# Two convolution layers by involution: which tiles of a column are multiplied 64 channels at a time, and which queue issues the window copies

## The chip, the core and the metric

The kernel runs on one core of a Trainium2 chip. A core has five engines with a queue each: TensorE (PE, matrix products; its weight loads are shown apart as PEld), VectorE (DVE), ScalarE (ACT), GpSimd (POOL) and SyncE (SP, which here only issues DMA transfers). Each engine works through its instructions in program order and waits on semaphores for the others. Products are written to PSUM, which is used here as four pairs of banks of 512 float32 per partition. The metric is the device time of one execution in microseconds; less is better.

## The reference

The input is 4 images of 256 channels and 56 x 56 points. Four residual layers follow, each on a group-normalised input. The change touches the code of layers 0 and 2, which are involutions: every point has its own 7 x 7 kernel, shared by the 16 channels of a group, which is itself computed from the input.

```python
def _L0_conv_ref(x, reduce_w, reduce_b, span_w, span_b):
    patches = jax.lax.conv_general_dilated_patches(x, (K, K), (S, S), [(P, P), (P, P)])
    patches = patches.reshape(b, G, c // G, K * K, Ho, Wo)
    ...
    h = jnp.einsum('bchw,oc->bohw', xk, reduce_w) + reduce_b[None, :, None, None]
    kern = jnp.einsum('bchw,oc->bohw', h, span_w) + span_b[None, :, None, None]
    kern = kern.reshape(b, G, 1, K * K, Ho, Wo)
    out = (kern * patches).sum(axis=3)
    return out.reshape(b, c, Ho, Wo)
...
x = x + _L0_conv_ref(_gn(x), ...)
x = x + _L1_conv_ref(_gn(x), ...)
x = x + _L2_conv_ref(_gn(x), ...)
x = x + _L3_conv_ref(_gn(x), ...)
```

Layer 2 computes the same with a batch norm and a ReLU after the reduction and after the sum. Layer 1 is two 3 x 3 convolutions, layer 3 a gate by channel and by position.

## The kernel before

The three stages of the time are the first involution (to about 508 us of the span), the convolutions (to about 1250 us), and the second involution with the gates of layer 3 worked in between (to the end). The function `involution_layer` is run twice, with `layer` 0 and 2.

**Units and columns.** An involution goes through 8 units: 4 images by 2 blocks of 128 channels (the partitions). A unit first makes its tap matrices (`tap_matrices`, 32 groups of products at line 596, evicted to `kt` by DVE at line 615 and, each third, by ACT at line 608), and then goes through 7 columns, each 8 points wide and 56 high.

**Tiles.** A column is cut into 19 tiles of 3 x 8 = 24 points (the last has rows below the image). The input window of a tile is 9 x 14 = 126 points. With the window's points on the partitions, the involution of a tile is a product of `xw` (126 window points by channels) with `kt` (126 window points by 24 outputs, for each of 8 groups of 16 channels). As the groups have different taps, a product of 64 channels with the taps of 4 groups computes 4 x 24 values for each channel, of which only the 24 of its own group are wanted; one of 32 channels with 2 groups computes 2 x 24. A tile needs two products of 64 channels and 96 free elements, or four of 32 channels and 48 free elements. The wanted values are picked in the eviction, by as many passes as a product has groups: the first by ACT with a per-partition factor that is 1 or 0 (times the batch norm's scale in layer 2), the others by DVE, which add into the same tile `un` (line 657).

**`apply` (lines 625 to 664)** does a column by the table `O_PARTS`, two pairs of banks. The first pair has 5 tiles in each bank by products of 64 channels (30 rows of the image): 20 products, one ACT pass of 240 elements (line 650 in layer 0, 652 in layer 2), three DVE passes of 240. The second pair uses one bank, 9 tiles by products of 32 channels (26 rows): 36 products, one ACT and one DVE pass of 208. After each pair the result is added to the image: by POOL in layer 0 (line 662), by DVE with the ReLU in layer 2 (line 664).

**The windows.** For a column, a strip of the normalised image is written to `strip_sb` (POOL in layer 0, line 390; ACT in layer 2, line 388), PE transposes it in 7 pieces (line 405), ACT copies these to `xw` (line 417), and four DMA transfers copy `xw` to itself, shifted by 3 and by 6 rows, so that all 19 windows stand there (lines 423 and 425). SP issues all four in layer 2; in layer 0, POOL issues the second of the shift by 6 rows. `xw` has three buffers.

**The order** of each engine's instructions is the order of the program (`in_order`). In a unit's column loop it is: the column's products and evictions (`apply`), the transposes, copy and DMA transfers of a later column's windows (`next_windows`), the strip after that (`next_strip`), the statistics of the column before (line 1115), and pieces of other work placed by column: statistics of the next image (line 358) and the bottleneck products of the next image (line 468) in layer 0, and in layer 2 loads and POOL work of the gates. SP also issues the loads of the next images.

Of the kernel before, what the change touches and what calls it, by code (L numbers as in the profile page):

```python
# [10 lines left out]
F32 = mybir.dt.float32  # L11
AF = mybir.ActivationFunctionType
ALU = mybir.AluOpType
# [3 lines left out]
P = 128  # L17
B, C, H, W = 4, 256, 56, 56
# [5 lines left out]
G, GC = 16, 16  # L24
# [9 lines left out]
TY, TX = 3, 8  # L34
QY, QX = TY + KK - 1, TX + KK - 1
Q = QY * QX
NTY, NTX = -(-H // TY), W // TX
NT = NTY * NTX
TP = TY * TX
# [7 lines left out]

O_PARTS = ((4, (0, 5), 5, 30), (2, (10,), 9, 26))  # L50
NXW = 3


# [18 lines left out]
def net_kernel(  # L72
# [19 lines left out]
    nc = tc.nc  # L92
# [64 lines left out]
    bn = {}  # L157
# [141 lines left out]
    def involution_layer(layer, xin, xout, red, span, sb, xs_of, ahead=None, pending=None):  # L299

        with ExitStack() as es:
            wpool = es.enter_context(tc.tile_pool(name="iw", bufs=1))
            big = es.enter_context(tc.tile_pool(name="ibig", bufs=1))
            work = es.enter_context(tc.tile_pool(name="iwork", bufs=2))
            banks = es.enter_context(tc.tile_pool(name="banks", bufs=4, space=PSUM))

            def two_banks():

                return banks.tile([P, 2, 512], F32, name="ps")
# [82 lines left out]
            def window(ty):  # L392

                k, j = divmod(ty, TY)
                return (0, NSB, 2 * NSB - 1)[j] + k
# [3 lines left out]
            def begin_windows():  # L399

                flat = strips[len(xws)].rearrange("p h w -> p (h w)")
                ps = two_banks().rearrange("p i n -> p (i n)")
                begun_windows.append(ps)
                for k in range(NSB):
                    nc.tensor.transpose(ps[:Q, k * P : (k + 1) * P], flat[:, k * Q : (k + 1) * Q], ident_sb)  # L405

            def next_windows():

                if len(xws) == len(columns):
                    return  # L410
                if not begun_windows:
                    begin_windows()
                ps = begun_windows.pop()
                xw = work.tile([Q, NTY, P], F32, name="xw", bufs=NXW)
                xws.append(xw)

                nc.scalar.copy(xw[:, :NSB, :], ps[:Q, : NSB * P].rearrange("q (n c) -> q n c", n=NSB))  # L417

                n = NSB - 1
                for j in range(1, TY):  # L420
                    cut = TY * QX * j
                    at = window(j)
                    nc.sync.dma_start(xw[: Q - cut, at : at + n, :], xw[cut:Q, 0:n, :])
                    eng = nc.sync if layer == 2 or j == 1 else nc.gpsimd
                    eng.dma_start(xw[Q - cut : Q, at : at + n, :], xw[:cut, 1 : 1 + n, :])


            h_of = {}
# [196 lines left out]
            def apply(b, cb, kt, tx, xw):  # L625

                img = xs_of[b, cb].rearrange("p (h w) -> p h w", w=W)
                y0 = 0
                for ng, tys, nty, rows in O_PARTS:
                    pair = two_banks()  # L630
                    nb, m = len(tys), ng * GC
                    v = pair[:, :nb, : ng * nty * TP].rearrange("p i (e n) -> p i e n", e=ng)
                    for i in range(nb):
                        for k in range(nty):
                            ty = tys[i] + k
                            for j in range(P // m):
                                nc.tensor.matmul(  # L637
                                    v[m * j : m * j + m, i, :, k * TP : (k + 1) * TP],
                                    xw[:, window(ty), m * j : m * j + m],
                                    kt[:, ng * j : ng * j + ng, :, ty * NTX + tx, :],  # L640
                                    start=True,
                                    stop=True,
                                )
                    n = rows // nb * TX
                    o = [v[:, :, e, :n] for e in range(ng)]
                    un = work.tile([P, 2, O_PARTS[0][3] // 2 * TX], F32, name="un")
                    un = un.rearrange("p i n -> p (i n)")[:, : rows * TX]
                    part = un.rearrange("p (i n) -> p i n", i=nb)
                    if layer == 0:
                        nc.scalar.mul(part, o[0], bn["par"][ng][:, 0:1])  # L650
                    else:
                        nc.scalar.activation(  # L652
                            part, o[0], AF.Identity, bias=bn["t4"][:, cb : cb + 1], scale=bn["s4"][ng][:, 0, cb : cb + 1]
                        )
                    for e in range(1, ng):
                        s = bn["par"][ng][:, e : e + 1] if layer == 0 else bn["s4"][ng][:, e, cb : cb + 1]
                        nc.vector.scalar_tensor_tensor(part, o[e], s, part, ALU.mult, ALU.add)  # L657
                    dst = img[:, y0 : y0 + rows, tx * TX : (tx + 1) * TX]
                    y0 += rows
                    u = un.rearrange("p (r x) -> p r x", x=TX)  # L660
                    if layer == 0:
                        nc.gpsimd.tensor_tensor(dst, u, dst, ALU.add)  # L662
                    else:
                        nc.vector.scalar_tensor_tensor(dst, u, 0.0, dst, ALU.max, ALU.add)
# [304 lines left out]
            if layer == 0:  # L969
                place(hooks0, begin(), (1, 2, 4, 6, 7))  # L970
            else:
                since = mark()
                load_taps(0)
                nc.sync.dma_start(zb_sb, zb2_dram)
                next_strip()
                run(bottleneck(0))
                hooks0[3] = list(pending[0])
                for _ in range(NXW - 1):
                    next_windows()
                    next_strip()  # L980
                hooks0[7] = [next_windows, next_strip]
            if layer == 0:
                next_strip()
                for i in range(NXW):
                    hooks0.setdefault(2 + 5 * i, []).extend((next_windows, next_strip))
# [40 lines left out]
            for u, (b, cb) in enumerate(units):  # L1026
# [24 lines left out]
                if b + 1 < B:  # L1051
                    n = 16 if layer == 0 else (26, 21)[cb]
# [64 lines left out]
                for tx in range(NTX):  # L1117
                    if layer == 2 and u == len(units) - 1 and tx == NTX - 1:
                        column_sums(tx - 1)
                    for f in early[tx]:  # L1120
                        f()
                    apply(b, cb, kt, tx, xws[u * NTX + tx])
                    next_windows()
                    next_strip()
                    if tx > 0 and not (layer == 2 and u == len(units) - 1 and tx == NTX - 1):
                        column_sums(tx - 1)
                    for f in late[tx]:
                        f()
# [3 lines left out]
            b, cb, st, last_sums = prev  # L1132
# [636 lines left out]
```

## Time and profile before

| | |
|---|---|
| median of 3 runs | 1797.18 us (1792.46 to 1799.98) |
| the profiled execution, device time | 1791.96 us |
| its span, first to last instruction | 1790.2 us |
| mean granted TensorE clock | 0.983 |
| products of `apply` (L637) | 12,544 records, 340.4 us busy |
| eviction passes of DVE (L657) | 448, 102.5 us (layer 2) and 98.2 us (layer 0) |
| eviction passes of ACT (L652, L650) | 224, 59.6 us (layer 2) and 50.0 us (layer 0) |
| the copies `xw<-xw` | 392 issued by SP, 56 by POOL |

The profile is one execution, and the device time is 1.8 us more than its span. Times are in us, means of one instruction in ns. A float32 product is shown as two records of PE, and each has a weight load under PEld. In a row of the groups stand line, engine, operation, tile written and tiles read, their shapes, the number, the busy time, the mean of one, and behind the bar the engine's idle time before them and who ended it; "issue" is idle time for which the profile shows no wait. Matmuls are pipelined, so that the duration of one (about 0.2 us) is far above the step from one to the next.

### The profile page before, as it was taken

The numbers are of one execution on the slowest core, as the hardware profiler recorded it, in microseconds if no ns is written. First come the engines' busy times: TensorE is split into PE (matmuls) and PEld (weight loads), VectorE is DVE, ScalarE is ACT, GpSimd is POOL, SyncE is SP. The second block draws the span as 40 slices with busy tenths as digits, with TensorE's granted clock in tenths as the row PEclk, the third lists the DMA queues.
The fourth block names the chain that finished last, engine by engine and source line by source line (L and its number), as shares of the span: only waits on it lengthen the run. The fifth ranks groups of instructions, "written<-read, shape, count | busy, mean of one in ns | idle before, by whom it ended". The sixth has DMA issues, their size and how long they took to land.

```text
span 1790.2 us, 55795 instructions
## 1 busy us (share of the span) xinstructions
PE 1682.8 (94%) x24040; PEld 1469.8 (82%) x24040; DVE 1387.3 (77%) x2745; ACT 822.8 (46%) x1882; POOL 406.8 (23%) x627
## 2 busy tenths in 40 slices
PE   6999999999989999999999999999999899799887
PEld 4887888878878988898889888986887787688775
DVE  2777787776779988998899888985777687677675
ACT  2655556555642313231323122113768577577564
POOL 2224432344310000000000000001000464563572
PEclk9999999999989999999999999999999999999997
DMA  2445444644752112120112011122446667766753
GB/s 86 128 158 172 148 145 134 188 121 130 222 158 91 55 52 64 64 68 29 64 64 70 26 64 37 44 111 74 153 147 186 186 219 210 215 213 178 203 145 119
DMA packets 69043, 221.04 MB, mean 123 GB/s; under 512 B 13461, under 2 KB 23198, under 8 KB 65086
## 3 DMA queue, kind: packets, MB, share of 16 engines
q1 hardware_dynamic: 52302, 150.65, 27.1%
q0 software_dynamic: 14656, 64.77, 11.4%
q8 instruction: 190, 3.11, 0.7%
q10 hardware_dynamic: 1840, 2.05, 0.4%
q14 instruction: 55, 0.45, 0.1%
HBM read 80.91 MB, written 49.81 MB: 73 GB/s over the span
## 4 chain that ended last, share of the span: by engine, by line
PE 64%; DVE 20%; ACT 5%; issue 4%; DMA 4%; POOL 2%; SPq 1%; POOLq 0%; ACTq 0%; DVEq 0%
PE mm L1533 18%; PE ps L596 15%; PE ps L637 9%; PE mm L1451 9%; DVE kt L615 5%; PE mm L1422 5%; DVE un L657 4%; DMA xw<-xw 3%; PE ps L405 2%; PE ps L468 1%; ACT kt L608 1%; DVE st L1115 1%; DVE res L1526 1%; POOL strip_sb L390 1%; DVE xs L1385 1%
## 5 line engine op out<-in xcount | busy, mean ns | idle before, releaser
L596 PE MATMUL ps<-hp,z_sb 64*126 64x133 f32 x6144 | 387.6, 280 | 8.4 <-DVE kt L615 4.2
L637 PE MATMUL ps<-kt,xw 126*32 126x48 f32 (+1 forms) x12544 | 340.4, 223 | 53.3 <-issue 37.5
L596 PEld LDWEIGHTS ps<-hp,z_sb 64*126 64x126 f32 x6144 | 364.7, 186 | 27.7 <-DVE kt L615 6.2
L1533 PE MATMUL mm<-v,u_sb 128*128 128x280 f32 (+1 forms) x1728 | 383.5, 383 | 1.9 <-DVE u_sb L1264 1.5
L637 PEld LDWEIGHTS ps<-kt,xw 126*32 126x32 f32 (+1 forms) x12544 | 302.7, 118 | 99.4 <-issue 71.2
L615 DVE TENSOR_TENSOR kt<-ps,zb_sb 126x798 f32<-126x798 f32 x352 | 332.8, 980 | 63.8 <-PE ps L596 63.2
L1533 PEld LDWEIGHTS mm<-v,u_sb 128*128 128x128 f32 x1728 | 326.1, 189 | 56.3 <-DVE u_sb L1264 1.9
L608 ACT ACTIVATE kt<-ps,zb_sb 126x133 f32<-126x133 f32 x960 | 290.1, 492 | 101.0 <-PE ps L596 101.0
L1451 PE MATMUL mm<-v,u_sb 128*128 128x252 f32 (+1 forms) x936 | 209.7, 384 | 0.0
L1451 PEld LDWEIGHTS mm<-v,u_sb 128*128 128x128 f32 x936 | 176.5, 190 | 30.6 <-issue 0.8
L657 DVE SCALAR_TENSOR_TENSOR un<-ps,s,un 128x240 f32<-128x240 f32 x224 | 102.5, 458 | 90.6 <-ACT un L652 86.2
L1570 POOL DMA_DIRECT2D x<-xs x24 | 13.2, 549 | 680.1 <-DVE xs L1569 426.5
L657 DVE SCALAR_TENSOR_TENSOR un<-ps,par_sb,un 128x240 f32<-128x240 f32 x224 | 98.2, 456 | 77.7 <-ACT un L650 73.4
L1518 ACT ACTIVATE res<-xs,shift,norm_sb 128x1120 f32<-128x1120 f32 (+1 forms) x24 | 30.2, 1258 | 238.5 <-DVE xs L1569 107.3
L405 PE MATMUL ps<-ident_sb,strip_sb 128*126 128x128 f32 x784 | 113.2, 286 | 16.4 <-POOL strip_sb L390 10.5
L417 ACT COPY xw<-ps 126x896 f32<-126x896 f32 x112 | 101.4, 907 | 51.8 <-PE ps L405 43.3
L662 POOL TENSOR_TENSOR xs<-un,xs 128x240 f32<-128x240 f32 x112 | 72.3, 665 | 180.7 <-DVE un L657 180.5
L405 PEld LDWEIGHTS ps<-ident_sb,strip_sb 128*126 128x126 f32 x784 | 86.0, 143 | 28.0 <-POOL strip_sb L390 17.9
L652 ACT ACTIVATE un<-ps,bn_t,s 128x240 f32<-128x240 f32 x112 | 59.6, 538 | 101.4 <-PE ps L637 97.3
L1422 PE MATMUL mm<-xs,u_sb 128*128 128x126 f32 (+1 forms) x792 | 98.7, 277 | 2.1 <-DVE xs L1385 1.0
L650 ACT ACTIVATE un<-ps,par_sb 128x240 f32<-128x240 f32 x112 | 50.0, 448 | 104.0 <-PE ps L637 92.1
L1422 PEld LDWEIGHTS mm<-xs,u_sb 128*128 128x128 f32 x792 | 94.4, 191 | 3.5 <-DVE xs L1438 1.6
(256 smaller groups left out, 1905.8 us busy)
## 6 DMA issues: line engine op xcount, KB each, us to landing
xw<-xw SPq DMA_DIRECT2D x168, 252.0 KB
xw<-xw SPq DMA_DIRECT2D x224, 126.0 KB
xw<-xw POOLq DMA_DIRECT2D x56, 252.0 KB, 4.6
xs<-x SPq DMA_DIRECT2D x24, 560.0 KB
x<-xs POOLq DMA_DIRECT2D x8, 1568.0 KB
xs<-x SPq DMA_DIRECT2D x8, 1568.0 KB
xs<-in_x_dram SPq DMA_DIRECT2D x6, 1568.0 KB
x<-xs SPq DMA_DIRECT2D x6, 1568.0 KB
```

The lines of the kernel that those rows point to most:

```text
L405: nc.tensor.transpose(ps[:Q, k * P : (k + 1) * P], flat[:, k * Q : (k + 1) * Q], ident_sb)
L417: nc.scalar.copy(xw[:, :NSB, :], ps[:Q, : NSB * P].rearrange("q (n c) -> q n c", n=NSB))
L596: nc.tensor.matmul(ps[:Q, i, k * NT : (k + 1) * NT], z_sb[i * R : (i + 1) * R, cb * GB + g if layer == 0 else g, z0 : z0 + Q], hp[i * R : ...
L608: nc.scalar.activation(kt[:, g, pb, :, p], ps[:Q, i, k * NT : (k + 1) * NT], AF.Identity, bias=zb[:, p : p + 1],)
L615: nc.vector.tensor_tensor(kt[:, g, pb].rearrange("q t (i k) -> q t i k", i=2), ps[:Q, :, : PR * NT].rearrange("q i (k t) -> q t i k", k=PR ...
L637: nc.tensor.matmul(v[m * j : m * j + m, i, :, k * TP : (k + 1) * TP], xw[:, window(ty), m * j : m * j + m], kt[:, ng * j : ng * j + ng, :, ...
L652: nc.scalar.activation(part, o[0], AF.Identity, bias=bn["t4"][:, cb : cb + 1], scale=bn["s4"][ng][:, 0, cb : cb + 1])
L657: nc.vector.scalar_tensor_tensor(part, o[e], s, part, ALU.mult, ALU.add)
L662: nc.gpsimd.tensor_tensor(dst, u, dst, ALU.add)
L1422: nc.tensor.matmul(ps[:, co * m : (co + 1) * m], u[ci][:, co * P : (co + 1) * P], v2[:, e, : n // 2, ci * WT : (ci + 1) * WT], start=(ci = ...
L1451: nc.tensor.matmul(ps, u1_sb[:, ci, dy, k, co * P : (co + 1) * P], v[:, k, dy * NB + ci : (dy + n - 1) * NB + ci + 1 : NB, :], start=(j == 0),
L1533: nc.tensor.matmul(ps, u2_sb[:, ci, dy, k, co * P : (co + 1) * P], v[:, k, dy * NB + ci : (dy + n - 1) * NB + ci + 1 : NB, :], start=(j == 0),
```

## The change

`O_PARTS` now gives each bank of each pair as (groups of a product, first tile, tiles). The first pair is as before. The second pair has four tiles by products of 64 channels in its first bank and five by products of 32 in the second. A column has 28 products of 64 channels and 20 of 32, where it had 20 and 36. Where the two banks of a pair are alike they are evicted together; the second pair's are evicted one after the other, ACT once and DVE three times on 96 elements, then ACT and DVE once each on 120. The addition to the image remains one for each pair. In layer 0 the copy that POOL issued is issued by SP.

```diff
-O_PARTS = ((4, (0, 5), 5, 30), (2, (10,), 9, 26))
+O_PARTS = (((4, 0, 5), (4, 5, 5)), ((4, 10, 4), (2, 14, 5)))
...
-                    eng = nc.sync if layer == 2 or j == 1 else nc.gpsimd
-                    eng.dma_start(xw[Q - cut : Q, at : at + n, :], xw[:cut, 1 : 1 + n, :])
+                    nc.sync.dma_start(xw[Q - cut : Q, at : at + n, :], xw[:cut, 1 : 1 + n, :])
...
-                y0 = 0
-                for ng, tys, nty, rows in O_PARTS:
+                for banks_of in O_PARTS:
                     pair = two_banks()
-                    nb, m = len(tys), ng * GC
-                    v = pair[:, :nb, : ng * nty * TP].rearrange("p i (e n) -> p i e n", e=ng)
-                    for i in range(nb):
+                    for i, (ng, ty0, nty) in enumerate(banks_of):
+                        m = ng * GC
+                        v = pair[:, i, : ng * nty * TP].rearrange("p (e n) -> p e n", e=ng)
                         for k in range(nty):
-                            ty = tys[i] + k
+                            ty = ty0 + k
                             for j in range(P // m):
                                 nc.tensor.matmul(
-                                    v[m * j : m * j + m, i, :, k * TP : (k + 1) * TP],
+                                    v[m * j : m * j + m, :, k * TP : (k + 1) * TP],
                                     xw[:, window(ty), m * j : m * j + m],
                                     kt[:, ng * j : ng * j + ng, :, ty * NTX + tx, :],
...
-                    n = rows // nb * TX
-                    o = [v[:, :, e, :n] for e in range(ng)]
-                    un = work.tile([P, 2, O_PARTS[0][3] // 2 * TX], F32, name="un")
+                    tiles = sum(nty for _, _, nty in banks_of)
+                    rows = min(tiles * TY, H - y0)
+                    un = work.tile([P, 10 * TP], F32, name="un")
+                    same = banks_of[0][::2] == banks_of[1][::2]
+                    at = 0
+                    for i, (ng, _, nty) in enumerate(banks_of[:1] if same else banks_of):
+                        nb = 2 if same else 1
+                        v = pair[:, i : i + nb, : ng * nty * TP].rearrange("p i (e n) -> p i e n", e=ng)
+                        o = [v[:, :, e] for e in range(ng)]
+                        part = un[:, at : at + nb * nty * TP].rearrange("p (i n) -> p i n", i=nb)
+                        at += nb * nty * TP
+                        if layer == 0:
+                            nc.scalar.mul(part, o[0], bn["par"][ng][:, 0:1])
...
+                        for e in range(1, ng):
+                            s = bn["par"][ng][:, e : e + 1] if layer == 0 else bn["s4"][ng][:, e, cb : cb + 1]
+                            nc.vector.scalar_tensor_tensor(part, o[e], s, part, ALU.mult, ALU.add)
```

More of the change, by code (lines that the diff above doesn't have):

```diff
@@ L643, in apply @@
                                 )
-                    n = rows // nb * TX
-                    o = [v[:, :, e, :n] for e in range(ng)]
-                    un = work.tile([P, 2, O_PARTS[0][3] // 2 * TX], F32, name="un")
[L647 to L654, printed above, removed]
@@ L655, in apply @@
-                    for e in range(1, ng):
-                        s = bn["par"][ng][:, e : e + 1] if layer == 0 else bn["s4"][ng][:, e, cb : cb + 1]
-                        nc.vector.scalar_tensor_tensor(part, o[e], s, part, ALU.mult, ALU.add)
+                    y0 = banks_of[0][1] * TY
+                    tiles = sum(nty for _, _, nty in banks_of)
+                    rows = min(tiles * TY, H - y0)
+                    un = work.tile([P, 10 * TP], F32, name="un")
+                    same = banks_of[0][::2] == banks_of[1][::2]
@@ new lines, in apply @@
+                    at = 0
[7 more added lines that the diff above has]
+                            nc.scalar.mul(part, o[0], bn["par"][ng][:, 0:1])
+                        else:
+                            nc.scalar.activation(
+                                part,
+                                o[0],
+                                AF.Identity,
+                                bias=bn["t4"][:, cb : cb + 1],
+                                scale=bn["s4"][ng][:, 0, cb : cb + 1],
+                            )
+                        for e in range(1, ng):
+                            s = bn["par"][ng][:, e : e + 1] if layer == 0 else bn["s4"][ng][:, e, cb : cb + 1]
+                            nc.vector.scalar_tensor_tensor(part, o[e], s, part, ALU.mult, ALU.add)
@@ L658, in apply @@
                     dst = img[:, y0 : y0 + rows, tx * TX : (tx + 1) * TX]
-                    y0 += rows
-                    u = un.rearrange("p (r x) -> p r x", x=TX)
+                    u = un.rearrange("p (r x) -> p r x", x=TX)[:, :rows]
                     if layer == 0:
```

## The prediction

> **What bounds the kernel now.** I read the page first, then the groups of the product line with shapes kept apart, then one quiet column of each involution in the chain and the timeline, then the columns that stall.
>
> From the page:
>
> ```profile
> PE 1682.8 (94%) x24040; PEld 1469.8 (82%) x24040; DVE 1387.3 (77%) x2745; ACT 822.8 (46%) x1882; POOL 406.8 (23%) x627
> ...
> q8 instruction: 190, 3.11, 0.7%
> ...
> PE 64%; DVE 20%; ACT 5%; issue 4%; DMA 4%; POOL 2%; SPq 1%; POOLq 0%; ACTq 0%; DVEq 0%
> ```
>
> PE has the largest share, but 94% is a mean: the changed code runs only in the product columns, 112 stretches of 3 to 8 us. The queue named "instruction" and the 4% "issue" in the chain matter below. The groups of the product line and of the evictions:
>
> ```profile
> L637 PE MATMUL ps<-kt,xw 126*64 126x96 f32 x4480 | 228.9, 251 | 16.7 <-DMA xw<-xw 10.6 <-DVE un L657 3.5 <-issue 1.1
> ...
> L637 PE MATMUL ps<-kt,xw 126*32 126x48 f32 x8064 | 120.8, 207 | 36.6 <-issue 36.4
> ...
> L657 DVE SCALAR_TENSOR_TENSOR un<-ps,par_sb,un 128x240 f32<-128x240 f32 x168 | 78.3, 466 | 74.8 <-ACT un L650 70.9
> ...
> L657 DVE SCALAR_TENSOR_TENSOR un<-ps,par_sb,un 128x208 f32<-128x208 f32 x56 | 23.9, 427 | 2.9 <-ACT un L650 2.6
> ```
>
> Each float32 product is two records, so a column is 40 records of 64 channels (ten tiles) and 72 of 32 (nine tiles). Nearly all "issue" idle time, 36.4 us, stands before the 32-channel records. A quiet column of the first involution, by windows of line 637 (columns: stretch, its length, PE busy, weight loads busy, clock, DMA share, GB/s):
>
> ```profile
> 206.68:208.53 1.85, 1.85 (x40) 1.73 (x40) 1.00 0.75 231
> 208.53:209.51 0.98, 0.98 (x74) 0.84 (x72) 1.00 0.51 114
> ```
>
> Ten tiles by 64 take 1.85 us, nine by 32 take 0.98 us. The chain around it (start, length, what):
>
> ```profile
> 205.76 0.99 PE ps L405 x7
> 206.75 1.88 PE ps L637 x40
> ...
> 209.21 0.48 DVE un L657
> ...
> 211.43 0.52 POOL xs L662
> ...
> 212.00 0.55 POOL xw L425
> ...
> 212.59 1.01 POOL strip_sb L390
> ...
> 213.65 0.98 PE ps L405 x7
> ```
>
> From transposes to transposes is 7.89 us and spans two columns, so a quiet column of the first involution takes 3.92 us (column starts 206.68, 210.60, 214.56). It is bound by this loop, not by PE, whose own work is 3.7 us. In the second involution ACT makes the strip, and quiet columns start at 1281.66, 1285.33 and 1289.02: 3.68 us, PE alone. A column that stalls (1536.40 us) has its gap inside the 32-channel records:
>
> ```profile
> 1536.40 2.13 PE L637 MATMUL ps<-kt,xw 126*64 126x96 f32 x43
> 1539.23 0.98 PE L637 MATMUL ps<-kt,xw 126*32 126x48 f32 x69 [0.70 <-issue]
> ```
>
> I measured all such stalls from starts of successive product records over 0.3 us apart with no releaser: 42, with 46.0 us beyond the usual step (11.0 us in the first involution, 35.0 us in the second; 37 of them inside the 32-channel records). All but two end 1.2 to 1.6 us after the end of a packet of queue 8. From column to column the position inside the column moves by a fixed step of 7. So PE waits for its next page of instructions: 48,080 PE and weight-load records over 190 packets is 253 to a page.
>
> **The change part by part.** *PE.* Four tiles of a column go from 32 to 64 channels; the free columns streamed per tile stay 192. The row gives 0.185 us per 64-channel tile. For the others it is 0.98/9 = 0.109 us if everything scales; but 0.2 us of the 0.98 (the row's 207 ns) is the modelled end of the column's last product, which stands there once before and after: 0.78/9 = 0.087 us. So 4 x 0.076 = +0.30 to 4 x 0.098 = +0.39 us; I take 0.39, as the tail stays. All 56 columns of the second involution pay: 56 x 0.39 = +22 us (17 at the low end). In the first the loop hides part: 20 quiet columns go from 3.92 to 3.68 + 0.39 = 4.07, +0.16 each; 12 columns with bottleneck products and 8 last columns of a unit pay all; the 16 opening ones, set by a similar eviction chain, +0.04. 3.2 + 4.7 + 3.1 + 0.6 = +12 us.
>
> *The loop through POOL.* It loses the 0.55 us copy issue (L425) and gains DVE work before POOL's second addition. There is no row for 96 or 120 elements; from 427 and 466 ns at 208 and 240 a straight line has 1.22 ns an element, so 290 and 319 ns. Bounds: 192 and 213 ns (proportional to 466) and 427. Three of 96 and one of 120 replace one of 208: 3 x 290 + 319 - 427 = +0.76 us DVE a column, 0.36 to 1.28. Following the rows above, DVE ends at 210.69 + 1.27 = 211.96, the addition takes 0.65, the strip 1.01, and the transposes come at 213.76 instead of 213.65: +0.05 a column, so the loop is shorter than PE's new 4.07 and stops binding. Without L425's removal it would be 4.2 and cost another 3 us over the quiet columns.
>
> *DVE elsewhere.* Second involution: three 240s with gaps 1.48, four small 1.2, the two residual operations 0.79, statistics 0.62, edge clears 0.06: 4.2 us against PE's 4.07. Its banks are four pairs deep, so a lag of 0.1 a column mostly rides along: bounds 0 to 56 x 0.15 = 8, I take +4. In the three first-involution units that also gather four statistics after their first column, DVE's second column ends 0.8 us later and its successor follows: +1.2 each, 3.6. At the 16 joins the first tap evictions (L615) queue behind 0.76 us more DVE while PE arrives only 0.39 later; bounds 0 to 0.4 x 16 = 6, I take 2. The last column has no cover: +1. Together +10 (bounds 2 to 19).
>
> *ACT.* One eviction of 208 becomes 96 and 120: +0.27 us (first) and +0.35 (second), by the slopes of L650 (435, 462) and L652 (524, 552 ns). It lies beside PE: ACT has 2 us of work in 4.07, or 3.4. In bottleneck columns of the second involution ACT has 5.9 against PE's 5.9; no extra beyond PE's.
>
> *SP and POOL.* 56 issues leave POOL (565 ns each) and add 782 ns each to SP: 4 x 0.78 = 3.1 us a column, under 4.07. Behind them on SP stand the next column's copies, which wait for ACT's L417 anyway, and block loads, issued during the taps. A copy now starts some 0.8 us later, and has two columns, 8 us, until use; 3.1 and a landing of 4.6 us fit barely. The second involution already does this at 3.68 a column and its quiet columns show no wait. Cost 0, up to 56 x 0.3 = 17 if the landing slips.
>
> *Instruction pages.* A column issues 2 x 112 + 14 = 238 PE and weight-load records; after, 2 x 96 + 14 = 206. At 253 to a page, a page lasts 253/238 x 3.68 = 3.9 us now and 253/206 x 4.07 = 5.0 after: each fetch has 1.1 us more. Taking 1.1 off each of the 42 stalls leaves 1.0 and 11.6 us: a gain of 33 us. Bounds: 0 (the fetch delay grows with the queues) and 46.
>
> The Trainium skill, "Runtime: NRT & Kernel Launch", section on instruction fetch mechanics, says that the sequencer fetches the next 16 KiB while it executes the present one and that crossing is "mostly hidden". By it the gain would be about nothing and the sum some +44. The 36.4 us of the row say that it is not hidden here, and I go by the row.
>
> *Sum.* 22 + 12 + 10 - 33 = +11 us on the profiled execution's 1791.96 (span 1790.2 and 1.8 around it): 1803. The median of the three runs is 5.2 above that execution, so I set 1808 beside 1797.2.
>
> **Rivals.** *Pages stop stalling altogether and DVE stays hidden:* -46, PE by its low bound (17 + 9), DVE +2: -18, 1779; with PE at 0.39, -10, 1787. For it: median stall in the first involution is 0.65 us, below 1.1. Against: seven in the second exceed 2 us, with DMA shares of 0.8. *Stalls remain* because fetches wait behind copies that are spread no thinner: gain 8 instead of 33, +36, 1833. For it: long stalls fall where DMA is busiest; against: fewer pages are fetched. *VectorE or the SP queue takes over:* DVE at its upper bound +9 and half the 17 of late copies, about +18 over the forecast, 1826. It decides once DVE passes 4.07 by more than the banks hold, or a landing takes over 5 us. That the change doesn't do what it says is excluded by the instruction order, which has 28 and 20 products and no POOL issue.
>
> **How the numbers follow.** Forecast 0.45 (1799 to 1819); stalls all gone 0.27; stalls remain 0.15; VectorE or SP 0.13. About 0.5%, 9 us, can be told from no change: below 1788 or above 1806. The first rival is nearly all faster (0.25, with 0.02 same); of the forecast 0.17 is same, 0.02 faster and 0.26 slower; the rest slower. Faster 0.27, same 0.19, slower 0.54. Range 1780 to 1834 leaves out the ends of the rivals.
>
> **What would show it.** Quiet columns: second involution 4.07 us, first 4.07 with no strip wait before the transposes. 64-channel records 56 in 2.6 us, 32-channel ones 40 in 0.6 us. "Issue" idle before 32-channel products about 10 us, 160 to 180 packets on queue 8. DVE busy up by 80 us. Copies' waits no longer than now. The prediction is wrong if quiet columns stay at 3.7 (then PE's price is wrong), or if stalls of over 1 us are as many as now.

## The result and the profile after

The changed kernel takes 1894.26 us (median of 4 runs, 1891.4 to 1901.87) against 1798.58 us for the kernel before, run beside it: a ratio of 1.0527, 95% interval 1.0493 to 1.056. Slower was forecast, but by 0.6%, not by 5.3%. The profiled execution took 1891.71 us with a span of 1889.9, 99.7 us longer than the span before.

From the page of the changed kernel, which answers to the first lines shown of before:

```profile
PE 1734.2 (92%) x22248; PEld 1517.2 (80%) x22248; DVE 1478.7 (78%) x3081; ACT 837.7 (44%) x1994; POOL 381.7 (20%) x571
...
q8 instruction: 176, 2.88, 0.6%
...
PE 56%; DVE 25%; ACT 8%; DMA 5%; issue 4%; SPq 1%; POOL 1%; ACTq 0%; POOLq 0%; DVEq 0%
```

PE's share of the chain falls from 64% to 56%, DVE's and ACT's rise by 5 and 3 points. PE became busier by 51 us (1682.8 to 1734.2), but the span grew by 100: PE waits more. The groups of the product line (L635 now) and of DVE's passes over the second pair (L666 now; the rows of layer 2):

```profile
L635 PE MATMUL ps<-kt,xw 126*64 126x96 f32 x6272 | 319.2, 256 | 36.8 <-DMA xw<-xw 20.9 <-DVE un L666 14.3
...
L635 PE MATMUL ps<-kt,xw 126*32 126x48 f32 x4480 | 72.3, 209 | 0.0
...
L666 DVE SCALAR_TENSOR_TENSOR un<-ps,s,un 128x96 f32<-128x96 f32 x168 | 52.9, 315 | 4.2 <-ACT un L657 0.2
...
L666 DVE SCALAR_TENSOR_TENSOR un<-ps,s,un 128x120 f32<-128x120 f32 x56 | 19.2, 343 | 29.1 <-ACT un L657 29.1
```

The 36.4 us of "issue" in front of the 32-channel records are 0.0 now: the stalls for instruction pages have gone altogether. DVE's small passes take 315 and 343 ns where a straight line gave 290 and 319, 0.1 us more in a column. The first is a gain and the second is small; neither explains 95 us. The view of the waits does (engine, line and tile that wait, whom for, us in total, times, longest):

```profile
ACT un L657 <- DVE un L666: 136.3, 56, 3.2
...
ACT un L655 <- DVE un L666: 100.9, 56, 3.7
```

Once in each of the 112 columns, ACT's eviction waits for DVE, 237 us in all. In the kernel before, the same view has one row of this kind, with 2.6 us:

```profile
ACT un L652 <- DVE un L657: 2.6, 3, 1.5
```

The timeline of one quiet column of the second involution shows where (start, length, engine, line, operation; in brackets the idle time before it):

```profile
1333.09 0.86 ACT L657 ACTIVATE un<-ps,bn_t,s 128x240 f32<-128x240 f32 x2
...
1333.66 1.47 DVE L666 SCALAR_TENSOR_TENSOR un<-ps,s,un 128x240 f32<-128x240 f32 x3 [0.64 <-ACT un L657]
...
1335.50 1.02 DVE L666 SCALAR_TENSOR_TENSOR un<-ps,s,un 128x96 f32<-128x96 f32 x3
1336.55 0.45 ACT L657 ACTIVATE un<-ps,bn_t,s 128x120 f32<-128x120 f32 x1 [2.60 <-DVE un L666]
1336.90 0.90 ACT L417 COPY xw<-ps 126x896 f32<-126x896 f32 x1
...
1337.69 1.05 ACT L388 ACTIVATE strip_sb<-xs,norm_sb 128x784 f32<-128x784 f32 x1
...
1338.63 0.87 ACT L657 ACTIVATE un<-ps,bn_t,s 128x240 f32<-128x240 f32 x2
...
1338.79 0.98 PE L405 MATMUL ps<-ident_sb,strip_sb 128*126 128x128 f32 x7 [1.44 <-ACT strip_sb L388]
```

ACT evicts the first pair and the first bank of the second (0.86 us), then stands for 2.60 us until DVE has made its three passes on the first pair, the residual operation and three passes on the 96 elements. Then come the 120 elements, the copy of the windows, the strip, and the next column. In the trace, the pass over the 120 elements starts 33 to 35 ns after the end of DVE's third pass over the 96, in all 112 columns. ACT's loop is 1338.63 - 1333.09 = 5.54 us, where quiet columns took 3.68. PE's products end at 1337.36 and its transposes wait for the strip until 1338.79.

The wait was made by the program: ACT's pass over the 120 elements writes another part of the same tile `un` that DVE is adding into, and stands after DVE's passes in the program. There ACT's pass over the 120 elements waits on DVE's semaphore in each of the 112 columns. The kernel before has one ACT pass for each tile `un`, ahead of DVE's, so that no pass of ACT stands behind DVE's additions to its own tile.

### The profile page after: what moved, and what is told of

Its sections match the earlier page's. It is cut to its first block, busy times and chain, and to the rows that moved or that the text cites. A ratio compares the mean times of both kernels' runs of the same rounds, so it can differ in the third digit from the quotient of the medians.

```text
span 1889.9 us, 52509 instructions
## 1 busy us (share of the span) xinstructions
PE 1734.2 (92%) x22248; PEld 1517.2 (80%) x22248; DVE 1478.7 (78%) x3081; ACT 837.7 (44%) x1994; POOL 381.7 (20%) x571
## 4 chain that ended last, share of the span: by engine, by line
PE 56%; DVE 25%; ACT 8%; DMA 5%; issue 4%; SPq 1%; POOL 1%; ACTq 0%; POOLq 0%; DVEq 0%
PE mm L1541 17%; PE ps L595 14%; DVE un L666 10%; PE mm L1459 10%; PE mm L1430 5%; DVE kt L614 4%; DMA xw<-xw 4%; PE ps L635 4%; ACT xw L417 2%; ACT un L657 2%; ACT hp L486 2%; DVE xs L672 1%; DVE st L1123 1%; ACT un L655 1%; ACT kt L607 1%
## 5 line engine op out<-in xcount | busy, mean ns | idle before, releaser
L595 PE MATMUL ps<-hp,z_sb 64*126 64x133 f32 x6144 | 393.9, 280 | 25.7 <-DVE un L666 12.4
L635 PE MATMUL ps<-kt,xw 126*64 126x96 f32 (+1 forms) x10752 | 382.3, 237 | 36.8 <-DMA xw<-xw 20.9
L635 PEld LDWEIGHTS ps<-kt,xw 126*64 126x64 f32 (+1 forms) x10752 | 348.4, 128 | 80.0 <-issue 56.3
L666 DVE SCALAR_TENSOR_TENSOR un<-ps,s,un 128x240 f32<-128x240 f32 x392 | 150.6, 384 | 114.7 <-ACT un L657 106.8
L666 DVE SCALAR_TENSOR_TENSOR un<-ps,par_sb,un 128x240 f32<-128x240 f32 x392 | 145.6, 383 | 70.9 <-ACT un L655 62.5
L657 ACT ACTIVATE un<-ps,bn_t,s 128x240 f32<-128x240 f32 x168 | 76.4, 477 | 181.9 <-DVE un L666 136.3
L655 ACT ACTIVATE un<-ps,par_sb 128x240 f32<-128x240 f32 x168 | 65.0, 389 | 168.4 <-DVE un L666 100.9
L149 POOL TENSOR_TENSOR norm_sb<-norm_sb,mhalf 128x1 f32<-128x1 f32 x32 | 19.8, 620 | 420.1 <-DVE norm_sb L148 420.1
```

Source lines behind the costliest of these rows:

```text
L595: nc.tensor.matmul(ps[:Q, i, k * NT : (k + 1) * NT], z_sb[i * R : (i + 1) * R, cb * GB + g if layer == 0 else g, z0 : z0 + Q], hp[i * R : ...
L635: nc.tensor.matmul(v[m * j : m * j + m, :, k * TP : (k + 1) * TP], xw[:, window(ty), m * j : m * j + m], kt[:, ng * j : ng * j + ng, :, ty ...
L657: nc.scalar.activation(part, o[0], AF.Identity, bias=bn["t4"][:, cb : cb + 1], scale=bn["s4"][ng][:, 0, cb : cb + 1],)
```

## The experiments

### ACT's passes first

The same work, with the order of the program changed: all ACT passes of a pair, then its DVE passes.

```diff
                         for e in range(1, ng):
                             s = ...
-                            nc.vector.scalar_tensor_tensor(part, o[e], s, part, ALU.mult, ALU.add)
+                            adds.append((part, o[e], s))
+                    for part, oe, s in adds:
+                        nc.vector.scalar_tensor_tensor(part, oe, s, part, ALU.mult, ALU.add)
```

> Only the order of the evictions is changed: the ACT passes of both banks of a pair stand in the program before the DVE passes, so that ACT's pass over the second bank no longer waits for DVE's three passes over the first. Theory A (that wait is what cost the 95 us, because it holds ACT's copy of the windows and its strip behind it): quiet columns of the second involution fall from 5.54 us to about 4.1, of the first to about 4.0, and the time to 1785 to 1815 us. Rival B (DVE's 0.95 us more work in a column sets it): the time stays above 1870. Rival C (half and half, the SP issues or PE's longer products being the rest): 1830 to 1860.

Measured: 1818.4 us, ratio 1.0114 (1.0071 to 1.0158). 76 of the 96 us are gone, with no instruction of PE, DVE, ACT or POOL added or removed. Of ACT's waits for DVE's additions, 3.3 us are left:

```profile
ACT un L657 <- DVE un L668: 3.3, 3, 1.5
```

Its timeline, a quiet column of the second involution:

```profile
1297.10 0.77 ACT L657 ACTIVATE un<-ps,bn_t,s 128x96 f32<-128x96 f32 x2 [0.72 <-PE ps L635]
1297.77 0.91 ACT L417 COPY xw<-ps 126x896 f32<-126x896 f32 x1
...
1298.56 1.06 ACT L388 ACTIVATE strip_sb<-xs,norm_sb 128x784 f32<-128x784 f32 x1
...
1300.07 0.98 PE L405 MATMUL ps<-ident_sb,strip_sb 128*126 128x128 f32 x7
```

Both small passes stand together, the copy follows at once, and PE waits for nothing before its transposes. Quiet columns take 4.02 us in both involutions (PE's own time, forecast as 4.07). Theory A holds for most of the loss; its range of 1785 to 1815 was missed by 3 us. Where the rest lies (20 us by the medians, 26 us by the spans of the two profiled executions) is listed below, stage by stage. Rival B falls: DVE does the same passes here.

### The wait alone, in the kernel before, and its control

To see the wait without PE's, DVE's or the pages' part, the old tiles are kept, and only the second pair's eviction is cut in pieces of 96 and 112 elements:

```diff
-                    if layer == 0:
-                        nc.scalar.mul(part, o[0], ...)
+                    cuts = [(0, n)] if nb == 2 else [(0, 96), (96, n)]
+                    for c0, c1 in cuts:
+                        sub = part[:, :, c0:c1]
+                        if layer == 0:
+                            nc.scalar.mul(sub, o[0][:, :, c0:c1], ...)
...
+                        for e in range(1, ng):
+                            nc.vector.scalar_tensor_tensor(sub, o[e][:, :, c0:c1], s, sub, ALU.mult, ALU.add)
```

> The kernel before, its tiles, products and queues untouched; only the second pair's eviction is cut in two pieces of 96 and 112 elements of one tile, each ACT then DVE, so that ACT's second piece waits for DVE's pass on the first, which stands behind the first pair's three. Theory A (the wait alone costs most of the 95 us, since ACT's copy and strip stand behind it): 1840 to 1880 us, quiet columns of the second involution at 4.5 to 5 us. Rival (the cost of the change was work, not the wait): one more short pass on ACT and on DVE, 0.3 us each where they have slack, at most 1810.

The control does the same pieces with both ACT passes ahead of DVE's.

> The control: the same two pieces, but both ACT passes stand before DVE's. Theory A: no wait, 1795 to 1812 us, quiet columns as in the kernel before. Rival: the same time as the run with the wait, within 10 us.

Measured: 1853.1 us with the wait, ratio 1.0284 (1.0241 to 1.0327); 1800.76 us without it, ratio 1.0025 (1.0 to 1.0049). Both lie in the ranges of theory A. Quiet columns of the second involution take 4.85 us with the wait and 3.7 without it. The waits of the first, two rows, and of the control, one:

```profile
ACT un L656 <- DVE un L661: 95.7, 59, 2.3
...
ACT un L654 <- DVE un L661: 62.3, 56, 2.6
...
ACT un L656 <- DVE un L663: 2.2, 3, 1.2
```

ACT waits for DVE as in the changed kernel, 158 us instead of 237; DVE makes one short pass on the first piece here, and not three. The order of one ACT instruction costs 52 us here, with the products and PE's instructions untouched.

### The SP issue alone, and undone

```diff
-                    eng = nc.sync if layer == 2 or j == 1 else nc.gpsimd
-                    eng.dma_start(xw[Q - cut : Q, at : at + n, :], xw[:cut, 1 : 1 + n, :])
+                    nc.sync.dma_start(xw[Q - cut : Q, at : at + n, :], xw[:cut, 1 : 1 + n, :])
```

> The kernel before with the second part of the change alone: SP issues all four copies in the first involution too; tiles and evictions as before. Theory A: the removal of 0.55 us from POOL's loop shortens quiet columns of the first involution from 3.92 us to at most 3.7, up to 20 columns, so 1790 to 1800 us. Rival (copies land late behind one another on SP): 1810 us or more, with waits on the copies in the first involution.

Measured: 1790.13 us, ratio 0.9962 (0.994 to 0.9983): faster than the kernel before by 0.4%, a small gain but outside the interval of no change, and the fastest version here that computes the reference. Theory A's range was 1790 to 1800. A quiet column of the first involution by the timeline of PE:

```profile
208.50 0.98 PE L405 MATMUL ps<-ident_sb,strip_sb 128*126 128x128 f32 x7
209.41 2.84 PE L636 MATMUL ps<-kt,xw 126*64 126x96 f32 x112
212.18 0.98 PE L405 MATMUL ps<-ident_sb,strip_sb 128*126 128x128 f32 x7
```

It takes 3.68 us from transposes to transposes, with none of the wait for the strip that made it 3.92. Some copies did come later: PE's waits for them in that stage went from 1.8 to 6.7 us, far from the rival's price.

> The changed kernel with the copy issued by POOL again in the first involution. Theory A: no more than 10 us from the changed kernel's 1894, slower rather than faster, as POOL's loop is longer. Rival (SP's issues cost much): below 1870.

With this line put back in the changed kernel: 1911.88 us, ratio 1.0632 (1.0586 to 1.0678), 18 us slower than the changed kernel. The sign was expected, the size not (at most 10). The time lies in the columns of the first involution, 281.8 us where the changed kernel has 264.6. The same issue costs more than twice the 7.5 us of before. There, only 3.92 - 3.68 = 0.24 us of its 0.55 showed in a quiet column, as PE's own work took the rest of the time; that DVE's longer passes lay more of it bare here is argued and not shown.

### All tiles by 32 channels

```diff
-O_PARTS = (((4, 0, 5), (4, 5, 5)), ((4, 10, 4), (2, 14, 5)))
+O_PARTS = (((2, 0, 10),), ((2, 10, 9),))
```

with ACT's passes first and `same` false for a pair of one bank.

> All 19 tiles by products of 32 channels (ten in one pair, nine in the next), evictions as before in kind, SP issuing all copies. PE's products in a column fall to about 1.7 us and DVE's passes to two, but a column has 318 PE and weight-load records, 1.26 pages of 253. If pages are fetched one at a time with some 3.5 us each (theory of the pages): columns of 4.3 us and more, stalls inside nearly every column, 1830 to 1880 us. If pages cost little: columns of 3.0 to 3.4 us set by ACT and by POOL's loop, 1710 to 1750 us.

Measured: 1893.46 us, ratio 1.052 (1.0464 to 1.0577), 13 us above the range of the theory of the pages and far from the other. The columns take 5.0 us on average in the first involution and 5.9 in the second. The group of its products:

```profile
L635 PE MATMUL ps<-kt,xw 126*32 126x48 f32 x17024 | 270.3, 222 | 209.8 <-issue 200.9 <-DMA xw<-xw 3.1 <-DVE xs L674 2.6
```

PE is 112 us less busy with products than in the changed kernel (270.3 against 382.3 us), and idle for 201 us with nothing to wait for that the profile knows. So the stalls are not PE's work or a wait on an engine that the profile shows. They grow with the number of PE's instructions in a column: at 206 a column none in the changed kernel and 2.4 us with ACT first, at 238 a column 46 us in the kernel before, at 318 a column 222 us (stalls counted as in the prediction). The number is not all that counts: with the same 238, the kernel with the pieces has 27 us with the wait and 32 without it. A column of 64-channel products alone would have fewest pages, one of 32 alone least work; the kernel before lies between. All tiles by 64 was not run.

### Without the gate's transfers

Two kernels leave out the loads of the gate's chunks (filled with a constant) and all but 8 of 448 columns of their stores, the old tiles with SP's issues and the new tiles with ACT's passes first.

```diff
-                nc.gpsimd.dma_start(xs, xout[b][cb][:, at])
+                nc.gpsimd.memset(xs, 0.5)
...
-                nc.gpsimd.dma_start(ov[b, cb][:, at], xs)
+                nc.gpsimd.dma_start(ov[b, cb][:, j * CR * W : j * CR * W + 8], xs[:, :8])
```

> The old tiles with all copies issued by SP, and without the loads and most of the stores of the gate's chunks (42 x 2 x 224 KB; the chunks are filled with a constant and 8 of 448 columns are stored, so the output is not the reference's). Theory (the long page stalls come from transfers that stand before the page): the 45 us of page stalls in the second involution fall to under 15, time 1735 to 1760. Rival (pages are late by themselves): 30 us or more of page stalls remain, time over 1765.

Measured: 1774.96 us. Page stalls in the second involution went from 37.4 us (the run with SP's issues, not the 45 of the expectation) to 8.8, as the theory had it. The time came out above its range, and above the rival's bound of 1765: with 28.6 us of stalls fewer, the time is 15 us shorter. What took the rest is open.

> The new tiles with ACT's passes first, and the same loads and stores of the gate left out. Theory: the 25 us of waits for copies in the second involution go too (under 6), and what is left against the old tiles without the gate's transfers is PE's and DVE's longer work in full: 35 to 55 us more than that run. Rival (copies are late because SP issues them late, not because of the traffic): 15 us or more of copy waits remain.

Measured: 1809.25 us, 34 us above the other (35 to 55 expected). Waits for copies in the second involution went from 25.2 to 9.9 us, so neither expectation was met. That the traffic causes these waits is not shown: with the old tiles, the same removal left them where they were (12.7 and 13.7 us). With the traffic, the new tiles with ACT first are 28 us above the old with SP's issues (1818.4 and 1790.13); the intervals are too wide to tell 28 from 34.

## Why the prediction was wrong

Where the 100 us are, by the starts and ends of the products in the traces (columns: from a unit's first product to its last; joins: from there to the next unit's first; us):

| | before | changed | ACT first |
|---|---|---|---|
| columns, first involution | 245.2 | 264.6 | 255.0 |
| joins, first involution | 186.8 | 196.1 | 191.7 |
| columns, second involution | 269.0 | 319.5 | 269.7 |
| joins, second involution | 210.3 | 227.4 | 219.3 |
| stalls for pages | 46.1 | 0.0 | 2.4 |
| waits for copies, in the products | 13.7 | 24.7 | 26.0 |

The columns of the table are one profiled execution each. The last two rows are parts of the first and third. The remainder of the span (start, convolutions, tail) grew by 3.4 us in the changed kernel and by 1.6 with ACT first.

**The step that failed** is the one on ACT: "It lies beside PE: ACT has 2 us of work in 4.07, or 3.4." This step counted ACT's busy time and took its passes as ready when PE was. The third pass, over the 120 elements, was not: by the program it waits for DVE, for 237 us in all, and behind it on ACT's queue stand the copy of the windows and, in the second involution, the strip, which PE waits for. ACT is busy for 838 us of 1890 and still sets the columns of the second involution. The wait was priced at nothing and measures 76 us (1894.26 - 1818.4). "DVE elsewhere" followed the same picture and let DVE's lag ride along in the banks. The prediction added up durations and took no account of what each instruction waits for. DVE's own work was sized well enough: its busy time rose by 91 us, where 80 were forecast. (The lower bounds of 192 and 213 ns for its small passes, called proportional to 466, should be 186 and 233; the sum of the four stays the same within 4 ns.)

**PE's price** was right: 0.39 us a column forecast, 0.34 measured (products of a quiet column from 2.83 to 3.17 us, quiet columns of 4.02 with ACT first).

**The pages** were right in sign and under-sized: 33 us of 46 were to go, 44 to 46 went. The term that was too small is the 1.1 us more for each fetch. In the changed kernel the wait also made the columns longer, but with ACT first, at 4.02 us, only 2.4 us of stalls are left. The Trainium skill ("Runtime: NRT & Kernel Launch", instruction fetch mechanics) calls these crossings mostly hidden; with 318 instructions of PE in a column the stalls sum to 222 us here, so the measurement decides against it for code this dense.

**Copies** were to be waited for no longer than now; with ACT first PE waits 12 us more for them (26.0 against 13.7). Whether the new tiles cause this is not shown. The control with the old tiles, in a profiled execution of 1815.16 us (its median is 1800.76), also has fewer page stalls and more waits for copies than the kernel before, as its groups show beside 10.6 us for copies and 36.4 of issue there:

```profile
L637 PE MATMUL ps<-kt,xw 126*64 126x96 f32 x4480 | 235.8, 255 | 44.4 <-DMA xw<-xw 34.6 <-DVE un L663 4.2 <-issue 3.7
...
L637 PE MATMUL ps<-kt,xw 126*32 126x48 f32 x8064 | 120.5, 210 | 22.6 <-issue 21.9 <-ACT strip_sb L388 0.3
```

In two stretches of the second involution, the kernel with ACT first shows (PE, weight loads, DVE, ACT, POOL busy; clock, DMA share, GB/s):

```profile
1428.00:1453.00 25.00, 19.67 (x425) 17.42 (x425) 18.22 (x47) 13.23 (x23) 17.35 (x26) 0.86 0.91 249
1692.00:1718.00 26.00, 20.20 (x424) 18.17 (x416) 17.98 (x47) 12.73 (x22) 17.51 (x25) 0.87 0.87 236
```

The transfers are busy for 87 to 91% of the time in these stretches, and for 61% over the whole second involution. That a stall removed on PE comes back there as a wait for copies is a reading that fits, and no experiment here separates it.

**The joins** were sized at 2 us and grew by 14 with ACT first (4.9 and 9.0), by 26 in the changed kernel: DVE leaves the columns behind PE, and the first tap evictions stand behind its passes. With ACT first, PE's tap products wait 25.8 us for DVE's tap evictions, where it was 10.4.

**SP's copies** at nothing: right for the time, as the run with SP's issues alone is 0.4% faster, and the loop through POOL was indeed what bound quiet columns of the first involution (3.92 us with POOL's issue, 3.68 without).

With the wait left aside, the forecast of +11 stands against +20. That it comes so close is in part luck, as errors of 10 us and more cancel: the pages gave 11 to 13 us more than forecast, the joins cost 12 more, and waits for copies, forecast as unchanged, cost 12.

The rivals: "stalls all gone" is what happened to the stalls, and the time still rose. "VectorE or the SP queue takes over" came nearest, but it decides by DVE's load, and the same load with another order gives 76 us back.

What stays open is whether a tile `un` of its own for the second bank would remove the wait without a change of order; this was not tried. The trace with ACT first suggests that the two parts of a tile are ordered as one: in none of the 112 columns does DVE's first pass over the 96 elements start before ACT's pass over the other 120 has ended (33 ns after it at the least), though the pass over the 96 that it needs had ended at least 0.28 us earlier.

## What to carry to other kernels

When a change splits one eviction into two on the same tile, look at which instructions wait and for whom before adding up durations: an engine that is 44% busy sets the pace if the instruction it holds waits and the next stage's inputs stand behind it. Put all passes of the engine that feeds other stages ahead of the passes of the engine that follows, in the program as well. Price a gain where it acts: in a stretch whose transfers are nearly always busy, a stall removed may come back in part as a wait for them, and one trace of each kernel is not enough to tell.

## What the runs showed of the hardware

PE can run out of instructions. Its stalls with no releaser end, but for a few, 1.2 to 1.6 us after the end of a packet of the instruction queue. They sum to 0 to 2.4 us at 206 PE instructions in a column, 46 at 238 in the kernel before, and 222 at 318; those of the second involution fell from 37.4 to 8.8 us when 19 MB of other transfers were taken away. In none of the ten traces do two packets of this queue start less than 3.3 us apart. With 253 instructions to a packet, that makes, as an estimate, at least 4.2 us for a column of 318 instructions, 3.1 for one of 238 and 2.7 for one of 206; quiet columns of the kernel before take 3.68.

A wait of PE can cost more than itself, as the granted clock falls in or after it. In the column that starts at 1442 us with ACT first, PE waits 1.9 and 2.4 us for copies (from the start of one record to the start of the next), and then its products run at half speed. Two windows of that kernel, there and in a quiet column (stretch, its length, busy time of PE, weight loads, DVE, ACT and POOL, clock, DMA share, GB/s):

```profile
1446.50:1449.00 2.50, 2.10 (x26) 2.13 (x28) 0.00 (x0) 0.00 (x0) 2.31 (x4) 0.50 0.88 288
1424.50:1427.00 2.50, 2.50 (x60) 2.38 (x63) 2.36 (x7) 2.45 (x5) 1.25 (x3) 1.00 0.81 193
```

The granted clock is 0.50 for 6.8 us, from 1444.6, and a pair of 64-channel records takes 160 ns where it takes 85 in the quiet column. With all tiles by 32, where PE stalls most, the granted clock is 0.50 for 172 us of the two involutions, against 14 us in the kernel before; so the stalls are not the whole loss of that run.
